# A two-layer decoder on one core: the last batch's shared expert and the first batch's way to transposed tokens move behind the conditional block

## The chip, the core and the metric

The kernel runs on one core of one Trainium2 chip as one launch. The metric is the device time of that launch in microseconds (us). A core has a matrix engine (PE, whose weight loads are listed apart as PEld), a vector engine (DVE), a scalar engine (ACT), GpSimd (POOL) and a queue engine that starts most transfers (SP). Each takes its instructions in the order in which they were written down for it, and waits where an instruction's input isn't there.

## The reference, cut to what matters

Four sequences (called batches here) of 512 tokens, 256 wide, go through two post-norm layers in float32:

```python
x = layernorm(x + L0_attn(x))            # attention over the 4 batches, 16 heads
x = layernorm(x + L0_xattn(x, ctx))      # one wide head against 1601 context rows
x = layernorm(x + L0_ffn(x))             # 16 experts, one for each token, and a shared expert
x = layernorm(x + L1_attn(x))            # causal, 16 heads of 16, rotary positions
x = layernorm(x + L1_xattn(x, ctx))      # 16 heads of 16 against the context
x = layernorm(x + L1_ffn(x))             # a soft decision tree of depth 8

def L0_ffn(x):
    logits = x @ w_router.T                          # 2048 tokens, 16 experts
    mask   = one_hot(argmax(logits))
    inputs = (sigmoid(logits) * mask).T[:, :, None] * x
    gate, up = split(inputs @ gate_up_proj)          # per expert, 256 -> 2 x 512
    routed = (up * silu(gate)) @ down_proj           # per expert, 512 -> 256
    shared = silu(x @ w_gate.T) * (x @ w_up.T) @ w_down.T   # every token
    return shared + routed.sum(over experts)
```

The change touches the third line, and the start of the fourth.

## The kernel before, in words

The program is three functions that run one after the other: `front()` (the first two lines of the model and the router), `experts()` (the third line without its norm) and `heads()` (that norm and the rest). Each builds a graph of nodes with `Plan.add` (`N` in the code) and calls `Plan.run`, a list planner. A node names an engine (or two, from which the planner chooses), an estimated cost, a due position, the nodes that it needs, and the buffers it takes and frees. The planner walks through its own estimated time; at each step it takes, among the nodes that can start soonest, the one with the smallest due position, and writes its instructions down. So it fixes the order on every engine before anything runs; on the chip only true data dependencies make an engine wait. Nodes that are named "none" hold a buffer; "dma" nodes stand for a transfer's time in the planner only.

In `experts()` the tokens are sorted by expert into tiles of 128 rows. 24 tiles (`NF`) are always done, in `sorted_tiles`. For each tile, three indirect transfers on POOL fetch the expert's weights (`wgu`, `wdn`) and the tile's token rows (`xs`); DVE scales the rows by the router's score (line 837), PE transposes them (842), ACT copies them out (249), PE multiplies by the gate and up weights, ACT takes the silu (857), DVE multiplies (859), PE multiplies by the down weights, ACT or DVE copies the result out and SP stores it to the DRAM array `ys_dram` (871). All multiplications go through the helper `mm` and carry its line, 245, so the tile names tell them apart: `xsT,wgu` and `wdn,he` are a tile's, `xT,w_sgu` and `w_sdn,hs` are the shared expert's.

The shared expert needs only the tokens: for each batch, eight multiplications into one PSUM bank each (`up`), four silus on ACT (798), four products on DVE (800), four multiplications (`down`), and four additions into the token rows `X` on DVE (808). All four batches are in the same graph as the tiles, with due positions 5.5 apart, and tile t is due at 0.2 + t.

Up to seven more tiles can be needed, depending on the router; they stand in a conditional block of their own behind the graph:

```python
            with tc.If(tiles[0] > NF):
                sorted_tiles(more, range(NF, NS))
                more.run(tc)
```

In the profiled execution the block is passed over; every engine still evaluates the branch (line 902).

`heads()` opens pools of its own for SBUF and PSUM, over the memory that `experts()` used. Its graph begins with `begin(b, pos)` for the four batches: four indirect transfers on POOL gather the tokens' expert rows from `ys_dram` by `dest` (1321), DVE adds `X` (1329), and `norm` normalizes them: statistics (1249, 1250), an inverse root by twelve small DVE instructions (`inverse_root`, 1234 to 1240), the norm into `XB` (1257), eight transposes on PE (1272), two copies into `XT`, and an addition of a bias row to `XB` on POOL (1278). From `XT` come the projections of each head group, rotary positions, a redistribution by SP transfers into `qT` and `kT`, and a first pass of scores for the row maxima (1106, 1108). Ahead of the heads the graph also clears buffers (`clear`, `ones_behind`), loads a pattern into the key buffers (`keys_of`, 962) and loads the tree's weights into the memory of `w_sgu` (`fetched`, 1420), where they stay in four of the ten buffers for exponentials (`raw`) until two small products have used them. All of these wait, in the planner, for batch 0's gathers to be issued or landed (`gathered`, `landed`).

Of the kernel before, what the change touches and what calls it, by code (L numbers as in the profile page):

```python
# [8 lines left out]
I32 = mybir.dt.int32  # L9
# [178 lines left out]
def act(n):  # L188
    return 0.1 + n * 0.833e-3


def dve(n):
    return 0.16 + n * 1.05e-3
# [11 lines left out]
def tile_decoder(ctx: ExitStack, tc: tile.TileContext, a, out):  # L205
# [37 lines left out]

    def mm(out, lhsT, rhs, c=0, n=1):
        nc.tensor.matmul(out, lhsT, rhs, start=c == 0, stop=c == n - 1)  # L245

    def copy(on, dst, src):
        if on == "act":
# [400 lines left out]
    def experts():  # L649
        plan = Plan()  # L650
        N, hold = plan.add, plan.hold
        with tc.tile_pool(name="mi", bufs=1) as mi, tc.tile_pool(name="mip", bufs=1, space=PSUM) as mip:
# [128 lines left out]
            sr = N("dve", 0.4, 0.0, sources, [so], free=[so])  # L781


            shared = [[] for _ in range(NB)]
            for b in range(NB):
                pr = 0.5 + 5.5 * b - (0.0 if b == 0 else 0.0)
                hs = hold("hs", pr)
                hid = []
                for f in range(4):
                    banks = []  # L790
                    for w in range(2):
                        def up(n, b=b, f=f, w=w):
                            for c in range(2):
                                mm(ONE[n.slot], w_sgu[:, c, w * F + f * P : w * F + (f + 1) * P], XT[b][:, c, :], c, 2)

                        banks.append(N("pe", cost_mm(1024), pr + f, up, [hs], take=["one"]))
                    s = hold("ss", pr + f)
                    e = N("act", act(512), pr + f, lambda n, s=s, p=banks[0]: nc.scalar.activation(
                        SS[s.slot], ONE[p.slot], AF.Silu), [s, banks[0]], free=[banks[0]])
                    hid.append(N("dve", dve(512), pr + f, lambda n, s=s, p=banks[1], hs=hs, f=f: nc.vector.tensor_tensor(  # L800
                        HS[hs.slot][:, f, :], SS[s.slot], ONE[p.slot], ALU.mult), [e, banks[1]], free=[banks[1], s]))
                for k in range(4):
                    def down(n, k=k, hs=hs):
                        for f in range(4):
                            mm(ONE[n.slot][:, :D], HS[hs.slot][:, f, k * P : (k + 1) * P], w_sdn[:, f, :], f, 4)

                    p = N("pe", cost_mm(1024), pr + 4 + k, down, hid, take=["one"], free=[hs])
                    shared[b].append(N("dve", dve(256), pr + 4 + k, lambda n, i=4 * b + k, p=p: nc.vector.tensor_tensor(
                        X[i], X[i], ONE[p.slot][:, :D], ALU.add), [p], free=[p]))


            gu_rows = a["L0_ffn_gate_up_proj"].rearrange("e p c n -> (e p) (c n)")
# [89 lines left out]
            with tc.If(tiles[0] > NF):  # L902
                sorted_tiles(more, range(NF, NS))
                more.run(tc)

    experts()


# [3 lines left out]
    def heads():  # L912
        plan = Plan()
        with tc.tile_pool(name="h1", bufs=1) as h1, \
# [41 lines left out]
            def ones_behind(n, t):  # L956
                nc.gpsimd.memset(t[:, :, :, HD : HD + 1], 1.0)
# [270 lines left out]

                return N("dve", 0.45, pe_, scaled, [r, cat], free=[po, rs]), cat

            def inverse_root(t, var):

                v, s, y = t[:, 0, :], t[:, 1, :], t[:, 2, :]
                nc.vector.tensor_scalar_add(v, var, EPS)
                nc.vector.tensor_single_scalar(y.bitcast(I32), v.bitcast(I32), 1, ALU.arith_shift_right)
                nc.vector.tensor_scalar(y.bitcast(I32), y.bitcast(I32), -1.0, 1597463007.0, ALU.mult, ALU.add)
                for _ in range(3):
                    nc.vector.scalar_tensor_tensor(s, y, -0.5, y, ALU.mult, ALU.mult)
                    nc.vector.tensor_tensor(s, s, v, ALU.mult)
                    nc.vector.scalar_tensor_tensor(y, s, 1.5, y, ALU.add, ALU.mult)  # L1240

            def norm(b, pos, y, parts, row=None):


                st, mv, sd = hold("lst", pos), hold("lmv", pos), hold("lsd", pos)
                stats = []
                for kq in range(4):
                    def stat(n, kq=kq):
                        nc.vector.bn_stats(ST[st.slot][:, kq, :], YY[y.slot][:, kq, :])  # L1249
                        nc.vector.bn_aggr(MV[mv.slot][:, kq, :], ST[st.slot][:, kq, :])  # L1250

                    stats.append(N("dve", 0.6, pos, stat, [parts[kq], st, mv]))

                rc = N("dve", 2.3, pos, lambda n: inverse_root(SD[sd.slot], MV[mv.slot][:, :, 1]), [sd, *stats], free=[st])
                norms = []
                for kq in range(4):
                    norms.append(N("dve", 0.47, pos, lambda n, kq=kq: nc.vector.tensor_scalar(  # L1257
                        XB[b][:, kq, :], YY[y.slot][:, kq, :], MV[mv.slot][:, kq, 0:1], SD[sd.slot][:, 2, kq : kq + 1],
                        ALU.subtract, ALU.mult), [rc]))
                plan.frees(norms[-1], [y, mv, sd])  # L1260
                if row is None:
                    for h in range(2):
                        i = 4 * b + 2 * h
                        N("sp", 0.4, pos, lambda n, i=i, h=h: nc.sync.dma_start(
                            out[i * P : (i + 2) * P, :].rearrange("(k p) d -> p k d", p=P),
                            XB[b][:, 2 * h : 2 * h + 2, :]), norms[2 * h : 2 * h + 2])
                    return
                xt = []
                for c in range(2):
                    def turn_x(n, c=c):  # L1270
                        for kq in range(4):
                            nc.tensor.transpose(ONE[n.slot][:, kq * P : (kq + 1) * P],  # L1272
                                                XB[b][:, kq, c * P : (c + 1) * P], ident)

                    px = N("pe", 0.46, pos, turn_x, norms, take=["one"])
                    xt.append(N("act|dve", (act(L), dve(L)), pos, lambda n, c=c, px=px: copy(
                        n.on, XT[b][:, c, :], ONE[px.slot]), [px], free=[px]))
                rw = N("pool", pool(1024), pos, lambda n: nc.gpsimd.tensor_tensor(  # L1278
                    XB[b], XB[b], rows[:, row : row + D].unsqueeze(1).to_broadcast([P, 4, D]), ALU.add), xt)
                added[b] = rw  # L1280
                return xt

            def finish(cross, b, pos, cats, cat):
# [16 lines left out]
                for h in range(2):  # L1300
                    def proj(n, h=h):
                        for kq in (2 * h, 2 * h + 1):
                            for c in range(2):
                                mm(ONE[n.slot][:, (kq % 2) * D : (kq % 2 + 1) * D], CT[ct.slot][:, c, kq, :], wo[:, c, :], c, 2)

                    po = N("pe", cost_mm(4 * D), pos, proj, cc, take=["one"])
                    prods.append(po)
                    a_ = N("dve", dve(512), pos, lambda n, h=h, po=po: nc.vector.tensor_tensor(  # L1308
                        YY[y.slot][:, 2 * h : 2 * h + 2, :], ONE[po.slot].rearrange("p (k n) -> p k n", k=2),
                        XB[b][:, 2 * h : 2 * h + 2, :], ALU.add), [po, y, added[b]], free=[po])  # L1310
                    parts += [a_, a_]
                plan.frees(prods[-1], [ct])
                return norm(b, pos, y, parts, R_W2 if cross else R_O2)
# [1 line left out]
            def begin(b, pos):  # L1315
# [3 lines left out]
                for kq in range(4):  # L1319
# [1 line left out]
                    g = N("pool", 0.98, pos, lambda n, i=i, kq=kq: nc.gpsimd.indirect_dma_start(  # L1321
                        out=YY[y.slot][:, kq, :], out_offset=None, in_=ys_dram,
                        in_offset=bass.IndirectOffsetOnAxis(ap=dest[:, i : i + 1], axis=0)), [y])
                    if b == 0:
                        gathered.append(g)
                    g = N("dma", 0.4, pos, None, [g])
                    if b == 0:
                        landed.append(g)
                    parts.append(N("dve", 0.44, pos, lambda n, i=i, kq=kq: nc.vector.tensor_tensor(
                        YY[y.slot][:, kq, :], YY[y.slot][:, kq, :], X[i], ALU.add), [g]))  # L1330
                return norm(b, pos, y, parts, R_O1)
# [1 line left out]
            def tree(b, pos, after):  # L1333

                parts = []
                for h in range(2):
# [58 lines left out]
                    if h == 0:  # L1395
                        y = hold("y", pos, [co])
                    a_ = N("dve", dve(512), ph + 0.1, lambda n, h=h, p=p: nc.vector.tensor_tensor(
                        YY[y.slot][:, 2 * h : 2 * h + 2, :], ONE[p.slot].rearrange("p (k n) -> p k n", k=2),
                        XB[b][:, 2 * h : 2 * h + 2, :], ALU.add), [p, y, added[b]], free=[p])
                    parts += [a_, a_]  # L1400
                norm(b, pos + 1.2, y, parts)

            added = [None] * NB
            gathered, landed = [], []
            done = [begin(b, 4.0 * b - 5.0) for b in range(NB)]
            cleared = N("pool", 1.5, -1.5, clear, gathered)
            emptied = N("dve", 0.6, -4.9, lambda n: nc.vector.memset(ACC[0], 0.0))
            keyed = keys_of(slice(0, L), 0.8, -3.0, landed)
            keyed2 = keys_of(slice(L, LC), 1.6, 3.0, landed)
            framed = [N("pool", 0.4, -1.5 + k, lambda n, k=k: ones_behind(n, VV[k]), gathered) for k in range(2)]  # L1410


            raw = [hold("pe", -5.0) for _ in range(4)]
# [5 lines left out]
                for k, w in enumerate(("w_fq", "w_fr", "w_flT", "w_fo")):  # L1419
                    nc.sync.dma_start(two(k), a[w].rearrange("(c p) n -> p c n", p=P))  # L1420

            fw = N("dma", 2.5, -1.0, None, [N("sp", 2.7, -1.0, fetched, [*raw, *landed])])
            tree_ready = []
            for k, dst in enumerate((w_gate, w_leaf)):
                def both(n, k=k):
# [124 lines left out]
```

## Time and profile before

| | |
|---|---|
| time, median of 3 runs | 1726.19 us (1723.04 to 1727.55) |
| the profiled execution, its own time | 1728.98 us |
| its span, first to last instruction | 1727.2 us |
| mean granted PE clock | 0.974 |
| PE busy | 1636.8 us (95%) |
| DVE busy | 1104.3 us (64%) |
| ACT busy | 759.5 us (44%) |
| POOL busy | 330.2 us (19%) |

`front()` runs to about 257 us, the tiles and the shared expert from there to 485 us, and `heads()` from there to the end. Times in the views are counted from the span's start. In a timeline row the first number is the start, the second the length of the merged group, and the bracket tells how long the engine was idle before it and what ended the wait. A PE multiplication of this kernel shows as two records.

### The profile page before, as it was taken

How to read it: one execution, taken by the hardware profiler on the slowest of the kernel's cores; microseconds unless marked ns; L12 is line 12 of the kernel's file. 1: busy time of each engine (PE TensorE's matmuls, PEld its weight loads, DVE VectorE, ACT ScalarE, POOL GpSimd, SP SyncE). 2: the span in 40 equal slices, each digit the busy share in tenths (PEclk: the TensorE clock that was granted, in tenths of full speed). 3: DMA queues.
4: the chain of work that ended last, by engine and by line, in shares of the span. 5: the costliest groups of instructions: out<-in, count | busy, mean ns of one | idle time of the engine just before them, and what ended most of it. 6: DMA issues, size and time to landing. Idle time of an engine off the chain costs nothing.

```text
span 1727.2 us, 28379 instructions
## 1 busy us (share of the span) xinstructions
PE 1636.8 (95%) x10756; PEld 856.2 (50%) x10756; DVE 1104.3 (64%) x2690; ACT 759.5 (44%) x1534; POOL 330.2 (19%) x503
## 2 busy tenths in 40 slices
PE   7889999999959999999999999999999999999995
PEld 4677776888834555545433334333334333343323
DVE  6998555111138876777866766776667766677715
ACT  0335551211112434434446556455554555545581
POOL 6652003432144544422000000100000000010000
PEclk8999999999979999999999999999999999999998
DMA  8101005886331000001000000000000100001000
GB/s 304 36 2 38 25 25 199 272 277 219 115 113 38 25 14 19 17 16 26 14 3 11 14 13 14 7 19 14 13 14 1 26 14 14 13 1 26 1 1 13
DMA packets 41275, 87.50 MB, mean 51 GB/s; under 512 B 7856, under 2 KB 26800, under 8 KB 38064
## 3 DMA queue, kind: packets, MB, share of 16 engines
q1 hardware_dynamic: 32304, 42.66, 9.1%
q0 software_dynamic: 8832, 43.00, 7.3%
q8 instruction: 86, 1.41, 0.3%
q14 instruction: 53, 0.43, 0.1%
HBM read 64.52 MB, written 8.26 MB: 42 GB/s over the span
## 4 chain that ended last, share of the span: by engine, by line
PE 65%; DVE 4%; ACT 1%; issue 1%; DMA 1%; POOL 0%; DVEq 0%; POOLq 0%; ACTq 0%
PE one L245 48%; PE acc L1190 14%; DVE junk L1108 2%; PE one L1210 1%; PE one L1142 1%; PE one L1272 1%; ACT w_sgu L1173 0%; PE one L1291 0%; DMA y<-ys_dram,dest 0%; DVE x L1257 0%; DVE lst L1249 0%; DMA ys_dram<-ye 0%; PE one L1381 0%; DVE y L1308 0%; DVE rt L1373 0%
## 5 line engine op out<-in xcount | busy, mean ns | idle before, releaser
L1106 DVE TENSOR_REDUCE mx<-one 128x1 f32<-128x512 f32 x768 | 486.4, 683 | 190.0 <-PE one L245 185.7
L245 PE MATMUL one<-qa,kT 32*128 32x512 f32 (+4 forms) x2176 | 515.4, 598 | 6.2 <-ACT w_sgu L1173 4.2
L245 PE MATMUL one<-kT,qT 32*128 32x512 f32 (+4 forms) x2560 | 502.2, 529 | 6.2 <-DVE mx L1106 2.6
L1173 ACT ACTIVATE w_sgu<-one 128x512 f32<-128x512 f32 (+2 forms) x510 | 278.6, 591 | 244.8 <-PE one L245 242.7
L245 PEld LDWEIGHTS one<-qa,kT 32*128 32x128 f32 (+1 forms) x2176 | 179.6, 182 | 204.3 <-issue 68.9
L245 PEld LDWEIGHTS one<-kT,qT 32*128 32x128 f32 x2560 | 190.6, 184 | 168.3 <-issue 47.9
L1190 PE MATMUL acc<-w_sgu,v 128*17 128x512 f32 (+4 forms) x1084 | 261.9, 566 | 0.0
L1173 ACT ACTIVATE pe<-one 128x512 f32<-128x512 f32 (+1 forms) x342 | 189.8, 602 | 102.2 <-PE one L245 101.6
L1278 POOL TENSOR_TENSOR x<-x,rows 128x1024 f32<-128x1024 f32 x12 | 28.3, 2361 | 808.3 <-PE one L1272 808.2
L1190 PE MATMUL acc<-pe,v 128*17 128x512 f32 (+1 forms) x748 | 179.5, 566 | 0.0
L1108 DVE CUSTOM_DVE_ANT_0 junk<-one,consts 128x128 f32<-128x128 f32 (+3 forms) x256 | 125.4, 490 | 35.1 <-PE one L245 12.0
L1190 PEld LDWEIGHTS acc<-w_sgu,v 128*17 128x17 f32 (+1 forms) x1084 | 34.2, 96 | 176.3 <-issue 162.8
L1173 ACT ACTIVATE w_sdn<-one 128x512 f32<-128x512 f32 (+2 forms) x172 | 89.9, 568 | 63.4 <-PE one L245 63.1
L245 PEld LDWEIGHTS e_one<-xsT,wgu 128*128 128x128 f32 x768 | 89.5, 192 | 3.8 <-issue 2.9
L245 PE MATMUL e_one<-xsT,wgu 128*128 128x128 f32 x768 | 89.6, 275 | 0.0
L1190 PE MATMUL acc<-w_sdn,v 128*17 128x512 f32 (+2 forms) x344 | 84.1, 568 | 0.0
L245 PE MATMUL one<-w_in,xT 128*128 128x512 f32 (+1 forms) x128 | 47.8, 527 | 13.5 <-DMA xT<-in_xT 12.2
L245 PE MATMUL e_one<-xT,w_sgu 128*128 128x512 f32 x128 | 59.8, 609 | 0.3 <-DVE lg L613 0.3
L859 DVE TENSOR_TENSOR he<-sg,e_one 128x512 f32<-128x512 f32 x24 | 16.5, 686 | 61.6 <-PE e_one L245 51.0
L555 ACT ACTIVATE pe<-one,nm 128x512 f32<-128x512 f32 x64 | 37.3, 596 | 27.4 <-DVE nm L547 27.3
L245 PE MATMUL one<-pT,ctxN 128*128 128x128 f32 (+1 forms) x416 | 49.0, 275 | 0.0
L245 PEld LDWEIGHTS one<-pT,ctxN 128*128 128x128 f32 (+1 forms) x416 | 48.2, 192 | 1.6 <-issue 1.2
(290 smaller groups left out, 2023.3 us busy)
## 6 DMA issues: line engine op xcount, KB each, us to landing
kT<-ku SPq DMA_DIRECT2D x64, 100.1 KB
qT<-qu SPq DMA_DIRECT2D x128, 32.0 KB
ctxN<-in_ctxN SPq DMA_DIRECT2D x4, 832.0 KB
ctxT<-in_ctxT SPq DMA_DIRECT2D x4, 800.5 KB
ys_dram<-ye SPq DMA_DIRECT2D x24, 128.0 KB
xT<-in_xT SPq DMA_DIRECT2D x16, 128.0 KB
x<-in_x SPq DMA_DIRECT2D x16, 128.0 KB
x_dram<-x SPq DMA_DIRECT2D x16, 128.0 KB
```

What stands on the lines that cost most here:

```text
L245: nc.tensor.matmul(out, lhsT, rhs, start=c == 0, stop=c == n - 1)
L555: nc.scalar.activation(PE_[w.slot][:, : k1 - k0], ONE[b.slot][:, : k1 - k0], AF.Exp, bias=NM[nm.slot][:, 1:2], accum_out=PS[sm_.slot][:, i ...
L859: h = N("dve", dve(512), pr, lambda n, s=s, p=banks[1], he=he: nc.vector.tensor_tensor(HE[he.slot].rearrange("p j t -> p (j t)"), SG[s.slo ...
L1106: nc.vector.tensor_reduce(MX[mx.slot][:, kq, j, m : m + 1], t, AX.X, ALU.max)
L1108: nc.vector.tensor_tensor_reduce(out=junk[:, : k1 - k0], in0=t, in1=m_qk[:, 384 - kq * P : 512], scale=1.0, scalar=NEG, op0=ALU.add, op1=A ...
L1142: nc.tensor.transpose(ONE[n.slot][:, kq * P : (kq + 1) * P], NM[nm.slot][:, kq].rearrange("p j r -> p (j r)"), ident)
L1173: nc.scalar.activation(PE_[e.slot][:kn, :w], ONE[s.slot][:kn, :w], AF.Exp, scale=HD**-0.5)
L1190: nc.tensor.matmul(ACC[acc.slot][32 * j : 32 * j + HD + 1, q0:], VV[v.slot][:kn, t, 4 * (g % 2) + j, :], PE_[exps[j ^ 2][0].slot][:kn, w : ...
L1210: nc.tensor.transpose(ONE[n.slot][:, kq * P : (kq + 1) * P], OO[o.slot][:, kq * P : (kq + 1) * P], ident)
L1272: nc.tensor.transpose(ONE[n.slot][:, kq * P : (kq + 1) * P], XB[b][:, kq, c * P : (c + 1) * P], ident)
L1278: rw = N("pool", pool(1024), pos, lambda n: nc.gpsimd.tensor_tensor(XB[b], XB[b], rows[:, row : row + D].unsqueeze(1).to_broadcast([P, 4, ...
```

## The change

Three things are done.

1. The shared expert's nodes become a function `shared_expert(plan, b, pr)`. The first graph of `experts()` calls it for batches 0 to 2, with due positions 7.5 apart in place of 5.5.
2. A third graph, `both`, is built behind the conditional block. It holds batch 0's gathers, norm, transposes and bias addition (what `begin(0)` and `norm` did in `heads()`) with the due position -1.0, writing into part of a weight buffer that is free by then, and the shared expert of batch 3 with due position 0.0 and up.
3. In `heads()`, `begin` runs for batches 1 to 3 only. Batch 0 has nothing left to wait for (`done[0]` is empty), and the clears and key patterns no longer depend on batch 0's gathers. The loads of the tree's weights depend, in the planner, on batch 1's transposed tokens instead.

```diff
-            shared = [[] for _ in range(NB)]
-            for b in range(NB):
-                pr = 0.5 + 5.5 * b - (0.0 if b == 0 else 0.0)
+            def shared_expert(plan, b, pr):
+                N, hold = plan.add, plan.hold
                 hs = hold("hs", pr)
...
+            for b in range(NB - 1):
+                shared_expert(plan, b, 0.5 + 7.5 * b)
...
             with tc.If(tiles[0] > NF):
                 sorted_tiles(more, range(NF, NS))
                 more.run(tc)
+
+            both = Plan()
+            for name, slots_ in plan.pools.items():
+                both.pool(name, len(slots_))
+            N = both.add
+            y = WGU[0][:, 0].rearrange("p (k d) -> p k d", d=D)
+            st, mv, sd = et("st0", [P, 4, 6]), et("mv0", [P, 4, 2]), et("sd0", [P, 3, 4])
+            stats, norms, xt = [], [], []
+            for kq in range(4):
+                g = N("pool", 0.98, -1.0, lambda n, kq=kq: nc.gpsimd.indirect_dma_start(
+                    out=y[:, kq, :], out_offset=None, in_=ys_dram,
+                    in_offset=bass.IndirectOffsetOnAxis(ap=dest[:, kq : kq + 1], axis=0)))
+                g = N("dma", 1.5, -1.0, None, [g])
+                g = N("dve", 0.44, -1.0, lambda n, kq=kq: nc.vector.tensor_tensor(y[:, kq, :], y[:, kq, :], X[kq], ALU.add), [g])
...
+                stats.append(N("dve", 0.6, -1.0, stat, [g]))
+            rc = N("dve", 2.3, -1.0, lambda n: inverse_root(sd, mv[:, :, 1]), stats)
+            for kq in range(4):
+                norms.append(N("dve", 0.47, -1.0, lambda n, kq=kq: nc.vector.tensor_scalar(
+                    X[kq], y[:, kq, :], mv[:, kq, 0:1], sd[:, 2, kq : kq + 1], ALU.subtract, ALU.mult), [rc]))
+            for c in range(2):
...
+                p = N("pe", 0.46, -1.0, turn, norms, take=["one"])
+                xt.append(N("act|dve", (act(L), dve(L)), -1.0, lambda n, c=c, p=p: copy(
+                    n.on, XT[0][:, c, :], ONE[p.slot]), [p], free=[p]))
+            N("pool", pool(1024), -1.0, lambda n: nc.gpsimd.tensor_tensor(
+                XB[0], XB[0], rows[:, R_O1 : R_O1 + D].unsqueeze(1).to_broadcast([P, 4, D]), ALU.add), xt)
+            shared_expert(both, NB - 1, 0.0)
+            both.run(tc)
...
-            added = [None] * NB
-            gathered, landed = [], []
-            done = [begin(b, 4.0 * b - 5.0) for b in range(NB)]
-            cleared = N("pool", 1.5, -1.5, clear, gathered)
+            added = [[]] * NB
+            done = [[], *(begin(b, 4.0 * b - 5.0) for b in range(1, NB))]
+            cleared = N("pool", 1.5, -4.9, clear)
             emptied = N("dve", 0.6, -4.9, lambda n: nc.vector.memset(ACC[0], 0.0))
-            keyed = keys_of(slice(0, L), 0.8, -3.0, landed)
-            keyed2 = keys_of(slice(L, LC), 1.6, 3.0, landed)
-            framed = [N("pool", 0.4, -1.5 + k, lambda n, k=k: ones_behind(n, VV[k]), gathered) for k in range(2)]
+            keyed = keys_of(slice(0, L), 0.8, -3.0, [])
+            keyed2 = keys_of(slice(L, LC), 1.6, 3.0, [])
+            framed = [N("pool", 0.4, -1.5 + k, lambda n, k=k: ones_behind(n, VV[k])) for k in range(2)]
...
-            fw = N("dma", 2.5, -1.0, None, [N("sp", 2.7, -1.0, fetched, [*raw, *landed])])
+            fw = N("dma", 2.5, -1.0, None, [N("sp", 2.7, -1.0, fetched, [*raw, *done[1]])])
```

`inverse_root` moves to the top of the program unchanged, so that both places can call it.

## The prediction

> **What bounds the kernel now.** On the page PE is busy 95% of the span, DVE 64%, and 65% of the chain that ended last is PE: whatever keeps PE working is hidden, and only PE's holes, or PE time that becomes a hole, can move the end. First view: the chain of waits around the border between `experts()` and `heads()`.
>
> ```profile
> 485.20 3.63 DMA ys_dram<-ye
> ...
> 492.74 6.87 DMA y<-ys_dram,dest
> ...
> 504.56 0.14 issue
> 504.69 2.21 PE one L1272 x8
> 506.90 17.64 PE one L245 x64
> ```
>
> Between the last tile's store and the transposes of batch 0 there is no PE in the chain. Second view, busy time by stretch (span, then PE, PEld, DVE, ACT, POOL with instruction counts, granted clock, DMA share, GB/s):
>
> ```profile
> 324.00:344.00 20.00, 18.90 (x140) 17.88 (x138) 3.70 (x8) 3.56 (x8) 8.78 (x10) 1.00 0.84 278
> 464.00:484.00 20.00, 20.00 (x132) 18.58 (x131) 4.17 (x8) 2.59 (x6) 0.00 (x0) 1.00 0.04 15
> 484.70:504.70 20.00, 0.03 (x2) 0.04 (x1) 7.04 (x27) 0.37 (x1) 6.15 (x10) 0.64 0.61 209
> ```
>
> PE is full up to 484.7 and then idle for 20 us. The expert stage itself is PE-bound: its ten stretches of 20 us from 284 on have 197.1 us of PE in 200. Third view, the timeline: prices and releasers.
>
> ```profile
> 291.55 1.88 PE L245 MATMUL e_one<-xT,w_sgu 128*128 128x512 f32 x4
> 335.42 1.99 PE L245 MATMUL e_one<-wdn,he 128*128 128x256 f32 x8 [1.10 <-DVE he L859]
> 482.83 1.89 PE L245 MATMUL e_one<-wdn,he 128*128 128x256 f32 x8
> 490.22 0.95 POOL L1321 DMA_INDIRECT y<-ys_dram,dest  x1 [36.49 <-issue]
> 500.64 0.39 DVE L1329 TENSOR_TENSOR y<-y,x 128x256 f32<-128x256 f32 x1
> 504.69 2.21 PE L1272 MATMUL one<-consts,x 128*128 128x128 f32 x8 [19.97 <-DVE x L1257]
> 506.77 3.78 PE L245 MATMUL one<-xT,wq 128*128 128x512 f32 x4
> ```
>
> Fourth, two rows that tell how pools change hands: the longest waits, and the start of `experts()`.
>
> ```profile
> POOL ones L690 <- DVE best L619: 45.8, 1, 45.8
> 257.22 3.78 PE L245 MATMUL e_one<-xT,w_sgu 128*128 128x512 f32 x4 [0.32 <-DVE lg L613]
> ```
>
> The memset of `ones` has no input, yet it waited for the last DVE instruction of the stage before; the first PE instruction likewise for the copy that emptied the last bank. So a new pool's first writes wait for the old pool's last users.
>
> **Part by part.** T0 is the end of PE's work in the expert graph (before: 484.72, which is 482.83 + 1.89).
>
> *Taken out of the expert graph:* batch 3's shared expert. One `up` bank takes 1.72 us (from 291.55 to the next PE start, 293.27), eight take 13.8; the four `down` take 7.0 (284.37 to 291.34 for 32 records). Together 20.7 us of PE in a PE-bound stage: T0 becomes 464.0. Its four silus (0.60 each) and eight DVE instructions (0.69 and 0.42) lie beside PE, before and after.
>
> *What that filler covered.* Due positions 7.5 apart leave tiles 4 to 11 with little but tiles. There the trace has the like: seven tiles between 319.64 and 364.22, with only two `down` (3.5 us) between them, took 44.6 us for 7 x 5.51 of tile work (0.21 + 3.57 + 1.73): PE idled 2.2 us, in 1.1 us pieces as at 335.42, where DVE stood behind a late `xs` transfer. Eight such tiles give 2.5 us, and the last tile, whose silu and product nothing covers any more, about 1 (before, a `down` stood there). From above: if every filler-free tile took the 6.37 us of that stretch, 8 x 0.86 + 1 = 7.9; from below 0.5. DMA is no floor: 24 tiles of 1.84 MB and 2 MB of late weights at the 277 GB/s of that stretch are 167 us, from 275 to 442. I take 3: T0 = 467.0.
>
> *The branch.* PE's compare-and-branch of line 902 lasted 3.46 us, to 485.6, hidden in the hole. Now PE has work behind it, so 0.9 us show. If PE were held until 489.3, as SP was (T0 + 4.6), `up` would end at T0 + 18.4, 1.4 after the first norm that the next step finds: the wait there would vanish and the end move by under 1 us.
>
> *The new graph.* I follow the planner by its costs. Eight `up` fill PE until 13.75 in its time; gathers, additions, statistics, root, one product that slips in, and norms make the transposes ready at 14.7; the `down` need the fourth product, 15.4. So PE's order is eight `up`, two transposes, four `down`, and then `heads()`. On the chip: `up` ends at T0 + 0.9 + 13.8 = 14.7. The gathers can't come sooner after T0 than now: the store lands at +4.1, the first issue is at +5.5, the fourth at +9.3. They landed 6.9 us after issue, beside 3.4 MB that SP had started at 489 to 494; the gathers issued alone at 504.82 and 515.99 were used 2.7 and 3.0 later. SP's loads go into the new pool, whose first writes now wait until the shared expert has read its buffers, so I take 3.0 (bounds 2.7 and 6.9): +12.3. From the last addition to the last transpose was 6.26 us (500.64 to 506.90), plus 0.7 for the product, minus 0.5 since PE isn't cold: +18.7. PE waits 2.3 us for the first norm, and behind it stand the four `down` and all of `heads()`: +25.7.
>
> *Clock.* After the 2.43 us without PE work at 249.28 the granted clock was 0.50 from 252 until 261; after the hole the first four projections took 3.58 us to the next start, not 1.72. A wait of 2.3 us with half-empty transposes behind it looks like the first: 1.9 us more (0 from below), +27.6. The first projection waits for the last addition out of the old banks, 0.5: S = T0 + 28.1.
>
> The Trainium skill ("TensorE: Matmul & The Clock Gate", Part 1: The HAM clock gate) has PE throttled only after an idle window of about 3.4 us. By that the 2.3 us wait would leave the clock at full speed and the result would be 1.9 us lower; the trace speaks against it, with 0.50 after 2.43 us.
>
> *Balance at the start of `heads()`.* Before, 506.77 is T0 + 22.1. Now T0 is 20.7 - 3 earlier and S is 6.0 later: 11.7 us gained.
>
> *Moved past other queues.* Batch 0's four gathers, 20 small DVE steps, eight transposes, two copies and the 2.35 us bias addition are the same instructions. On POOL that addition now stands before the clears and batch 1's gathers; it ends by T0 + 21.1, before S, and costs nothing. But POOL's clears (2.0 us), batch 1's gathers and SP's key patterns, which ran inside the hole, now start at S beside the first projections. Their cover is the way from the first projection to the first scores, 17.7 us (506.77 to 524.45); that is now 1.9 shorter by the warm clock, and POOL's clears and first gather end about S + 3.7, where the first rotary product came at 4.6. What is late is batch 1: its tokens were transposed 19 us after the heads' first projection, and its transposes, its projections and the tree's two products (which the planner now puts behind it) filled PE's waits before 550. Without them at hand: 3.8 us of tree products and as much of projections, at most 7.6; at best the shorter way gains 2. I take a loss of 2.5, nearer the low end, as PE idled only 2.4 us there. The root's move and the lists change nothing.
>
> Sum: 11.7 - 2.5 = 9.2 off 1728.98, or 1719.8 in the profiled execution; its time was 2.8 above the median, so 1717.0.
>
> **Rivals.** (a) *The holes I priced don't open*: full clock through the wait, 0.5 lost in the stage, 1 gained at the heads' start: 9.2 + 1.9 + 2.5 + 3.5 = 17.1, giving 1709.1. For it: most tiles run without a gap even at 5.5 us. Against: the 0.50 after 2.43 us.
>
> (b) *SP's loads still meet the gathers*: landing 6.9, S 3.9 later but without more cold, about 3.4: 1720.4. For it: key buffers lie mostly over weight buffers that are free early. Against: the `ones` row.
>
> (c) *The filler was needed*: 7.9 lost in the stage and 5 at the start: 11.7 - 4.9 - 5 = 1.8, giving 1724.4, no change that can be told. For it: DMA share 0.84 to 0.89 in the sparse stretch.
>
> (d) *Slower: the exponentials' buffers.* Four of ten stay held until the tree's two products, now behind batch 1's tokens. Four exponentials go together, so with six buffers only two of the next four can run ahead: two wait, 1.2 us by their 0.60 each, three times a causal group, some 3.5 us. Before, the products ran at 521.77 and 530.65, the first exponential at 550.8. The loss decides once five groups run before the second product: 17.5 us, 1717.0 + 17.5 = 1734.5. Against: batch 1's tokens were there 23 us before that exponential.
>
> That the change doesn't do what it says isn't open: the graph is emitted behind the branch and PE has nothing else there.
>
> **The numbers.** A measurement of this kernel tells about 0.3% from no change, 5.2 us: 1721.0 to 1731.4. Forecast 0.47, (a) 0.20, (b) 0.11, (c) 0.13, (d) 0.09. Faster 0.78, same 0.13, slower 0.09. Time 1717.0. The best of all bounds is 11.7 + 1.9 + 2.5 + 2 = 18.1, or 1708.1; the range starts a little below and goes up to 1726.0, beyond (c), leaving out (d) and the edges.
>
> **What would show it.** T0 near 467; no idle stretch of 20 us, but one of 1 to 4 us before the eight transposes at T0 + 17; 32 records of `w_sdn,hs` right behind them, the first at half clock; gathers landing 3 us after issue; SP's key loads after the last `down`; the first head projection near 495. Wrong if T0 is above 473 (rival c), if gathers take 6 us (b), or if PE's waits in the first four head groups grow by over 8 us (d).

## The result, and the profile after

The changed kernel took 1719.6 us (median of 20 runs, lowest 1712.77), the kernel before 1727.55 (20 runs beside them). The ratio is 0.9957, with a 95% interval of 0.9941 to 0.9972: 7.4 us faster, by 4.8 to 10.2. One of the 20 runs took 3060.89 us and is left out of the ratio. Two later sets of runs of the same unedited file gave 0.9946 each. The forecast was 1717.0, with "faster" as the likeliest outcome. Of the 2.6 us between the forecast and the median, 1.4 are the kernel before, whose median was 1726.19 when the forecast was made. So the sum is nearly right. Its terms are not, as the rest shows: up to the first head projection the change gains 4 to 6 us more than forecast, and in the heads it loses 2 to 6 us more.

The profiled execution of the changed kernel took 1731.54 us (span 1729.8), which is longer than the one of before (1728.98, span 1727.2). Read alone, it would say "slower". Where its time went is the third part of this section.

**The border.** The chain of waits of the changed kernel (start, duration, what):

```profile
470.68 13.97 PE e_one L245 x32
...
485.53 6.92 PE e_one L245 x32
...
492.47 2.63 DMA kT<-in_keys
```

Where the chain of before had 20 us of store, gathers, additions and norms, it now has PE from 470.7 to 492.5. The timeline of PE shows what the three pieces are (start, duration, engine, line, operation, tiles, shapes; in brackets the idle time before it and what ended it):

```profile
467.11 1.99 PE L245 MATMUL e_one<-wdn,he 128*128 128x256 f32 x8 [0.85 <-DVEq L915]
470.68 13.97 PE L245 MATMUL e_one<-xT,w_sgu 128*128 128x512 f32 x32 [1.58 <-PEq L915]
484.49 1.04 PE L947 MATMUL e_one<-consts,x 128*128 128x128 f32 x8
485.36 7.07 PE L245 MATMUL e_one<-w_sdn,hs 128*128 128x256 f32 x32
493.00 1.96 PE L245 MATMUL one<-xT,wq 128*128 128x512 f32 x4 [0.56 <-issue]
```

T0 is 469.10 (467.11 + 1.99). The branch leaves 1.58 us open; then batch 3's eight `up`, the eight transposes of batch 0 without any wait, the four `down`, and the first head projection at T0 + 23.9. The 19.97 us hole is gone. The transposes could follow at once because the gathers were early, as the timeline of POOL and DVE shows:

```profile
472.28 0.95 POOL L929 DMA_INDIRECT wgu<-ys_dram,dest  x1 [30.84 <-issue]
477.55 0.43 DVE L933 TENSOR_TENSOR wgu<-wgu,x 128x256 f32<-128x256 f32 x1 [0.20 <-DMA wgu<-ys_dram,dest]
```

The first gather is issued at T0 + 3.2, not at T0 + 5.5 as before. The last norm ends at 484.41, just before the eighth `up` does (484.65).

**The first groups of heads.** Part of the gain is given back here. First the timeline of PE and DVE, then busy time by stretch (span; PE, PEld, DVE, ACT, POOL with counts; granted clock; DMA share; GB/s):

```profile
502.28 0.42 DVE L1365 TENSOR_TENSOR y<-y,x 128x256 f32<-128x256 f32 x1 [4.03 <-DMA y<-ys_dram,dest]
506.25 3.17 DVE L1365 TENSOR_TENSOR y<-y,x 128x256 f32<-128x256 f32 x1
511.00 0.67 DVE L1056 TENSOR_TENSOR rt<-one,consts 128x512 f32<-128x512 f32 x1
511.73 1.63 PE L245 MATMUL one<-kT,qT 32*128 32x128 f32 x4 [0.91 <-DVE rt L1056]
515.60 0.79 PE L245 MATMUL one<-kT,qT 32*128 32x128 f32 x2 [2.24 <-DVE mx L1159]
```

```profile
505.00:510.00 5.00, 4.61 (x14) 1.71 (x14) 4.86 (x6) 0.69 (x1) 3.97 (x5) 1.00 0.23 61
510.00:515.00 5.00, 2.44 (x11) 0.71 (x6) 4.56 (x18) 0.00 (x0) 1.26 (x1) 0.72 0.21 51
515.00:520.00 5.00, 4.40 (x12) 2.76 (x12) 4.50 (x15) 0.00 (x0) 2.41 (x3) 0.50 0.79 240
...
525.00:530.00 5.00, 5.00 (x25) 3.29 (x23) 3.15 (x12) 1.17 (x2) 3.28 (x2) 0.50 0.11 26
```

DVE is written down to do batch 1's additions ahead of the second rotary product (`rt`, line 1056) and the first maxima (`mx`, line 1159). It waits 4.03 us for the first gather, one addition takes 3.17 us, and PE, which has nothing else, waits 0.91 and 2.24 us for what stands behind. Batch 1's gathers now run beside SP's loads, and the second of them takes as long to land as batch 0's did before (chain of waits of the change):

```profile
497.29 6.87 DMA y<-ys_dram,dest
```

The granted clock falls to 0.50 between PE's two waits: 0.72 over the window from 510 to 515 means 2.8 us at half, so the fall is at 512.2. It lasts until 532.7, though PE is not idle at all after 515.6. The two waits cost 3.2 us; the clock costs more. Summed over the first 60 us after the first head projection (windows of 4 us; PE's busy time times one minus the granted clock), the clock took 12.4 us of PE's work in the changed kernel and 3.4 before, and PE idled 3.7 and 2.5 us. The difference is 10.2 us; the fourth group of heads is 10.8 us later than before, counted from the first projection. Up to group 15 the same sum, taken over the stretches at half clock, is 12.5, 16.8 and 14.1 us in the three profiles of the change and 5.2 before, while PE's waits are 8.6, 8.7 and 7.8 us and 7.8 before: what the heads lose is half clock.

What sets that half clock off is not shown. In the third profile of the change (`after_third`, busy time by stretch and timeline of PE) the clock falls at 507.1, 0.15 us after PE's long wait has begun, and PE had not waited for over 0.1 us since the first head projection at 488.72:

```profile
507.00:508.00 1.00, 0.00 (x0) 0.00 (x0) 0.84 (x5) 0.00 (x0) 0.17 (x1) 0.55 0.02 2
509.69 2.91 PE L245 MATMUL one<-kT,qT 32*128 32x128 f32 x8 [2.74 <-DVE mx L1159]
```

So the long wait isn't what brings the clock down there. Ahead of the fall PE runs the first scores, multiplications of 32 rows (`32*128`); whether these count is not tested.

**A spell of half clock.** The head groups 15 and 16 take 40.72 us from one to the next in the profile of before and 50.04 in this one. The same stretch in the profile of before, of the change, and of a second execution of the changed kernel:

```profile
830.00:840.00 10.00, 9.43 (x86) 5.81 (x86) 8.47 (x18) 1.79 (x5) 1.71 (x6) 1.00 0.09 12
```

```profile
830.00:840.00 10.00, 10.00 (x31) 3.69 (x27) 6.85 (x14) 0.97 (x2) 0.29 (x1) 0.50 0.26 45
```

```profile
830.00:840.00 10.00, 9.67 (x81) 5.97 (x82) 8.60 (x18) 2.31 (x5) 0.59 (x2) 1.00 0.35 56
```

In the second fence PE is as busy as in the others and does less than half as many multiplications. The three profiles of the unedited change show the spell in two cases and not in the third, with the same instructions in the same order. It costs 9.3 us, and that is why this profile is the longer one. All later profiles are therefore compared by stage:

| us | last `wdn,he` ends, from the stage's start | first head projection, from there | head group 1, from the projection | group 4 | group 15 | 15 to 16 | span |
|---|---|---|---|---|---|---|---|
| before | 227.8 | 22.1 | 59.5 | 111.5 | 308.4 | 40.7 | 1727.2 |
| after | 210.2 | 23.9 | 68.2 | 122.3 | 314.0 | 50.0 | 1729.8 |
| after_again | 208.5 | 24.2 | 66.2 | 121.2 | 317.3 | 40.7 | 1723.8 |
| after_third | 208.1 | 24.2 | 65.9 | 119.9 | 313.2 | 50.1 | 1724.9 |
| tokens_only | 228.5 | 16.8 | 64.1 | 119.0 | 310.9 | 40.7 | 1732.2 |
| shared_only | 208.3 | 39.7 | 59.7 | 111.5 | 307.2 | 50.1 | 1735.7 |
| tree_early | 209.8 | 23.9 | 61.8 | 116.8 | 311.0 | 40.7 | 1717.5 |
| tree_early_2 | 208.4 | 24.0 | 62.1 | 117.1 | 311.3 | 40.7 | 1716.0 |
| gather_5 | 209.1 | 24.2 | 60.5 | 116.8 | 313.6 | 40.7 | 1719.1 |
| tree_gather_5 | 208.9 | 23.9 | 56.7 | 109.6 | 308.2 | 46.8 | 1720.0 |
| tree_gather_5_2 | 207.7 | 23.9 | 59.2 | 112.0 | 312.1 | 40.7 | 1714.6 |
| spacing55 | 209.1 | 26.1 | 65.8 | 119.9 | 313.1 | 50.1 | 1730.3 |

The stage's start is DVE's copy of the router's logits (line 613 before, 624 after), the end of a `wdn,he` record is T0, and a head group is marked by its reciprocal of the row sums (`rs`). For the profile of the change the table adds up so: 2.0 later at the stage's start, 15.8 gained up to the first projection, 5.6 lost up to group 15, 9.3 in the spell, 1.5 after group 16: 2.6 longer. For the second execution: +2.8, -17.1, +8.9, 0 and +2.0: 3.4 shorter.

### The profile page after: what moved, and what is told of

Same layout as the page of the kernel before. It is cut to its first block, busy times and chain, and to the rows that moved or that the text cites. A ratio compares the mean times of both kernels' runs of the same rounds, so it can differ in the third digit from the quotient of the medians.

```text
span 1729.8 us, 28387 instructions
## 1 busy us (share of the span) xinstructions
PE 1655.4 (96%) x10756; PEld 863.2 (50%) x10756; DVE 1101.9 (64%) x2690; ACT 758.9 (44%) x1534; POOL 330.5 (19%) x503
## 4 chain that ended last, share of the span: by engine, by line
PE 66%; DVE 4%; ACT 1%; issue 1%; DMA 1%; POOL 0%; DVEq 0%; ACTq 0%
PE one L245 48%; PE acc L1241 14%; DVE junk L1159 1%; PE e_one L245 1%; PE one L1261 1%; PE one L1193 1%; PE one L1312 1%; PE one L1331 0%; ACT w_sgu L1224 0%; DMA y<-ys_dram,dest 0%; DVE y L1365 0%; DVE lst L1289 0%; DVE x L1297 0%; DVE y L1348 0%; DVE rt L1408 0%
## 5 line engine op out<-in xcount | busy, mean ns | idle before, releaser
L245 PE MATMUL one<-kT,qT 32*128 32x512 f32 (+4 forms) x2560 | 515.2, 539 | 8.2 <-DVE mx L1159 3.0
L1224 ACT ACTIVATE pe<-one 128x512 f32<-128x512 f32 (+2 forms) x342 | 184.6, 587 | 105.6 <-PE one L245 104.7
L1241 PE MATMUL acc<-pe,v 128*17 128x512 f32 (+2 forms) x748 | 174.1, 551 | 0.0
L1159 DVE CUSTOM_DVE_ANT_0 junk<-one,consts 128x512 f32<-128x512 f32 (+3 forms) x256 | 125.4, 490 | 44.5 <-PE one L245 22.6
L1224 ACT ACTIVATE w_sdn<-one 128x512 f32<-128x512 f32 (+2 forms) x174 | 96.4, 600 | 67.4 <-PE one L245 67.1
L1241 PE MATMUL acc<-w_sdn,v 128*17 128x512 f32 (+3 forms) x352 | 90.6, 594 | 0.0
L245 PE MATMUL e_one<-xT,w_sgu 128*128 128x512 f32 x128 | 59.2, 609 | 1.9 <-PEq L915 1.6
L245 PE MATMUL e_one<-wdn,he 128*128 128x256 f32 x192 | 45.9, 382 | 5.1 <-DVE he L872 4.3
L245 PE MATMUL one<-ctxT,q 128*128 128x512 f32 (+1 forms) x128 | 49.4, 518 | 0.0
```

Of the source, the lines that this page charges most:

```text
L1159: nc.vector.tensor_tensor_reduce(out=junk[:, : k1 - k0], in0=t, in1=m_qk[:, 384 - kq * P : 512], scale=1.0, scalar=NEG, op0=ALU.add, op1=A ...
L1224: nc.scalar.activation(PE_[e.slot][:kn, :w], ONE[s.slot][:kn, :w], AF.Exp, scale=HD**-0.5)
L1241: nc.tensor.matmul(ACC[acc.slot][32 * j : 32 * j + HD + 1, q0:], VV[v.slot][:kn, t, 4 * (g % 2) + j, :], PE_[exps[j ^ 2][0].slot][:kn, w : ...
```

## The experiments

**The change again.** The unedited file was run beside the first experiments and once more beside the last.

> The changed kernel once more, nothing edited, for a second profile and a second measurement. My theory: the gain at the heads' first projection (15 to 16 us against before, counted from the start of the expert stage) and the loss in the first four head groups (5 to 9 us) come back in every profile, since they follow from the written order; the 9.3 us that the first profile of the change lost between head groups 15 and 16, and 1.8 us at group 29, do not come back, since the order there is like the one of before; the time is 0.2 to 0.7% under the kernel before. Rival: the step at group 16 is a property of the new order; then it is there again with 9 us and the span is again about 1730.

> The changed kernel unedited, on the same chip as the next two, so that they can be compared: 0.4 to 0.6% under the kernel before. If half-clock spells come by chance, its profile shows 40.7 or about 50 us between the ends of head groups 15 and 16, and nothing between by more than a partial spell.

Measured: 1721.98 against 1728.42 (0.9946, 0.9926 to 0.9966), and 1717.94 against 1727.95 (0.9946, 0.9921 to 0.9971). T0 and the first projection came back within 2.1 and 0.3 us, the late first group too (66.2 and 65.9). The spell between groups 15 and 16 was gone in one and there in the other, so the written order alone doesn't bring it.

**Each half alone.** The first keeps the new graph for the tokens only; the shared experts are all where they were.

```diff
-            for b in range(NB - 1):
-                shared_expert(plan, b, 0.5 + 7.5 * b)
+            for b in range(NB):
+                shared_expert(plan, b, 0.5 + 5.5 * b)
...
-            shared_expert(both, NB - 1, 0.0)
```

> Batch 0's way to transposed tokens is in the graph behind the branch as in the change, but all four batches of the shared expert stay in the first graph, 5.5 apart as before. My theory (the filling of PE's hole is what gains): PE ends the expert graph where it did before, idles about 14 us instead of 20, since the gathers meet no loads and start sooner, and then the first head groups lose what they lose in the change: 5 us gained, 5 to 9 lost, the time within 0.3% of before or slightly above. Rival (the early, quiet gathers are the gain and the shared expert's place does not matter): 0.4% under before, like the change.

Measured: 1730.42 against 1728.42 (1.0002, 0.9981 to 1.0022): nothing. The timeline of PE in `tokens_only`:

```profile
505.38 2.21 PE L947 MATMUL e_one<-consts,x 128*128 128x128 f32 x8 [13.91 <-DVE x L942]
508.26 3.51 PE L245 MATMUL one<-xT,wq 128*128 128x512 f32 x4 [0.68 <-ACT xT L260]
```

The hole is 13.9 us instead of 20, as nothing fills it, and the heads start with half clock. Of the 5.3 us won from T0 on, 2.4 are lost up to group 15 (7.6 at group 4) by the heads, which have the order of the change; the rest is within what the interval leaves open.

The second moves only the shared expert; batch 0's gathers stay in `heads()`, with the old dependencies.

```diff
-            y = WGU[0][:, 0].rearrange("p (k d) -> p k d", d=D)
...
-                XB[0], XB[0], rows[:, R_O1 : R_O1 + D].unsqueeze(1).to_broadcast([P, 4, D]), ALU.add), xt)
             shared_expert(both, NB - 1, 0.0)
...
-            done = [[], *(begin(b, 4.0 * b - 5.0) for b in range(1, NB))]
+            gathered, landed = [], []
+            done = [begin(b, 4.0 * b - 5.0) for b in range(NB)]
```

> Only the shared expert of batch 3 is in the graph behind the branch; batch 0's gathers and norm stay in the graph of the heads as before, with the old waits in the planner. My theory (a new pool's first writes wait for the old pool's last users): the gathers, whose target lies in the heads' pool, can't start before PE has read the last buffer of the shared expert, about 22 us after the expert graph's end; the 16.5 us from first gather to first projection then stand bare again, PE idles 15 to 17 us, and nothing is gained: within 0.3% of before, or up to 4 us slower. Rival (no such wait): the gathers start 3 to 6 us after the expert graph's end and are hidden beside the shared expert: about 10 us faster than before.

Measured: 1736.98 against 1728.42 (1.0031, 1.0007 to 1.0054), slower. T0 is as early as in the change, but the gathers wait (timeline of PE and POOL):

```profile
482.93 7.07 PE L245 MATMUL e_one<-w_sdn,hs 128*128 128x256 f32 x32
490.76 0.95 POOL L1332 DMA_INDIRECT y<-ys_dram,dest  x1 [50.86 <-DVE x L818]
505.18 2.21 PE L1283 MATMUL one<-consts,x 128*128 128x128 f32 x8 [15.18 <-DVE x L1268]
```

The first gather goes out at T0 + 23, released by the shared expert's last addition into `X` (line 818): it writes into the pool that follows. The 21 us of PE work moved behind the tiles only push the hole back. Counted from the stage's start, the first head projection comes 1.9 us earlier than before here, 4.6 in `tokens_only`, and 15.8 to 17.6 in the change: each half is there to let the other lie beside it. In time the two halves are worth 0 and -0.3% alone and +0.5% together. The hole doesn't explain the -0.3%: this profile is 3 us ahead of before at group 15, and it is longer by the spell (50.1) and by 2.3 us ahead of the stage. Whether the other runs of `shared_only` lose their time in the same way is not shown.

**The loss in the heads.** The theory after the result was that DVE's order makes PE wait there and that the clock multiplies it: the tree's two products, which PE had between 520 and 532 before, now come at 540 and 548, and batch 1's additions stand ahead of the first maxima, since the planner counts 0.4 us for a gather that lands 6.9 after its issue. Two edits, each for one of these, and both together:

```diff
-            fw = N("dma", 2.5, -1.0, None, [N("sp", 2.7, -1.0, fetched, [*raw, *done[1]])])
+            fw = N("dma", 2.5, -1.0, None, [N("sp", 2.7, -1.0, fetched, [*raw])])
```

> The change, but the loads of the tree's weights no longer depend on batch 1's tokens in the planner (only on their buffers), so they are issued with the key patterns and the two tree products can fill PE's first waits again, as before. My theory of the loss at the heads' start (PE lacks work there, idles and falls to half clock): 2 to 5 us faster than the change, first head group's end 3 to 6 us nearer to its start. Rival (DVE's order is the cause: batch 1's additions and norm stand before the rotary product and the first maxima): no more than 1 us from the change.

> The tree edit alone, again. If its first measurement (0.85% under before, interval 0.51 to 1.19) holds: 3 to 5 us under the change on this chip. Rival (that measurement, with six undisturbed runs, was on the lucky side and the edit is worth what its trace shows up to head group 15, 3 us in one profile and 6 in the other): 1 to 6 us; nothing if its half-clock spells are more frequent.

```diff
-                    g = N("dma", 0.4, pos, None, [g])
+                    g = N("none", 5.0, pos, None, [g])
```

> The change, but in the planner the gathers of batches 1 to 3 take 5.0 us to land (a pure delay) in place of 0.4 us on the planner's transfer engine; nothing else is edited. Theory A (DVE's order: the additions of batch 1 stand at the head of DVE's queue and wait for gathers that land 3 to 7 us after issue, with the rotary products and the first maxima behind them): the first scores and maxima come sooner, PE's waits of 1.5 and 2.2 us between 509 and 516 shrink, and the time is 2 to 5 us under the change's. Theory B (what PE lacks is work: the tree's two products): within 1 us of the change's.

> Both edits together: the tree's loads free of batch 1's tokens, and 5.0 us for the gathers of batches 1 to 3 in the planner. Theory A: 2 to 4 us under the kernel with the tree edit alone, so some 1.1% under the kernel before, with the first head group ending 59 to 60 us after the first projection as before the change. Theory B: the same as the tree edit alone, 0.85% under before.

> Both edits, again. By its trace (head group 15 ends 308.2 us after the first projection against 314.0 and 317.3 for the change, the rest alike but for spells) it should be 6 to 9 us under the change. By its first measurement (0.59% under before) 1 us. If the second holds again, the gain of the first head groups is given back by half-clock spells later in the heads, which its profile should show as a mean clock no higher than the change's.

Measured, each against the kernel before on its chip: `tree_early` 1718.64 against 1728.42 (0.9915, 0.9881 to 0.9949) and 1717.75 against 1727.95 (0.9933, 0.9908 to 0.9959); `gather_5` 1722.39 against 1731.66 (0.9948, 0.9929 to 0.9966); both together 1719.68 against 1731.66 (0.9941, 0.9917 to 0.9965) and 1716.75 against 1727.95 (0.9933, 0.9908 to 0.9958).

Both edits bring group 1 forward. It comes 4 to 6 us earlier with the tree's products early, 5 to 8 with the gathers' time told, 7 to 12 with both, where it is as early as before the change or earlier. In `tree_early` the products lie where PE has work to do anyway, and the wait for `rt` remains; with both edits two waits of 1.4 us remain, 2.2 and 1.4 in the repeat (timelines of PE, first `tree_early`, then `tree_gather_5`):

```profile
508.99 1.89 PE L245 MATMUL one<-w_sgu 128*128 128x256 f32 x8
515.91 2.99 PE L245 MATMUL one<-kT,qT 32*128 32x128 f32 x10 [3.00 <-DVE rt L1056]
```

```profile
515.16 0.69 PE L245 MATMUL one<-kT,qT 32*128 32x256 f32 x2 [1.44 <-DVE mx L1159]
517.26 3.13 PE L245 MATMUL one<-kT,qT 32*128 32x256 f32 x4 [1.41 <-DVE mx L1159]
```

Summed as above over 60 us, the clock took 12.4 us in the change (11.7 and 12.8 in its repeats), 10.0 in `tree_early` and in its repeat, 8.9 in `gather_5`, and 4.4 and 8.1 with both. But the time does not follow group 1. `gather_5` was expected to gain a few us and gained nothing over the change (0.9948 against 0.9946 and 0.9957): its group 15 is no earlier (313.6 against 313.2 to 317.3), so what it wins up to group 1 is given back by the fifteenth. The traces show where. From group 1 to group 15 PE waits 6.9 us in `gather_5` against 4.7 to 5.6 in the three profiles of the change, and the half clock takes 5.1 us of its work against 0 to 4.9; what is left is 241 us in each. Both edits together were expected at 1.1% below before and reached 0.6 to 0.7%: there PE waits 7.9 us in this stretch in both profiles, and the half clock takes 3.4 and 5.0. `tree_early` and the two together beat the kernel before in each of their four measurements; against the change on the same chip they were 3.3, 0.2 and 1.2 us lower, and their intervals overlap with the change's. That they are the fastest versions is likely and not settled.

**The spacing of the filler.**

```diff
-                shared_expert(plan, b, 0.5 + 7.5 * b)
+                shared_expert(plan, b, 0.5 + 5.5 * b)
```

> The change with the due positions of the three remaining shared experts 5.5 apart as before, in place of 7.5. My step: the stage loses about 3 us for lack of filler between the tiles; with 5.5 the filler is used up earlier and the last tiles run bare, where each costs 0.5 to 1.4 us more. Expected: the expert graph ends 0 to 4 us later, and the time is within 0.3% of the change's. Rival (the filler's place is worth nothing): no difference at the graph's end beyond 0.5 us.

Measured: 1719.6 against 1731.66 (0.9937, 0.9913 to 0.9961), not slower than the change. The expert stage ends at the same time (209.1 against 208.1 to 210.2). So the two spacings make no difference to the stage that can be told. The first projection is 2 us later after T0 here, and the timeline of PE shows why:

```profile
470.69 15.67 PE L245 MATMUL e_one<-xT,w_sgu 128*128 128x512 f32 x32 [2.10 <-PEq L915]
```

PE waited 0.85 us, multiplied for 2.0 us (the last `wdn,he`), and waited 2.10 us at the branch. Then the granted clock was 0.50 for 3.4 us, from 471.9, and the eight `up` took 15.67 us in place of 13.97.

## Why the prediction was right or wrong, point by point

*The filler taken out.* Right. 17.7 us were forecast (20.7 - 3); the stage is 17.6, 19.3 and 19.7 shorter in the three profiles, so the holes cost 3.1, 1.4 and 1.0. The stage's end in `shared_only` (208.3) and `spacing55` (209.1) says the same. Rival (c), with 7.9 lost in the stage, is out; the 5 us that it had lost at the start of the heads did come, for another reason (below).

*The branch.* Forecast 0.9 us open; measured 1.58, 1.88 and 1.85. Too small by up to 1.

*The new graph's order* was as derived: eight `up`, the transposes, four `down`, the heads.

*The gathers.* This is the first step that failed: "The gathers can't come sooner after T0 than now". They came at T0 + 3.2 instead of 5.5, because the last store landed sooner, 1.7 us after its issue by the list of transfers, where the chain of before had 3.63; why it landed sooner is open. With that the norms were ready before the eighth `up` was done, and the wait of 2.3 us and the cold clock behind it, 1.9, had no place. The first projection came at T0 + 23.9 to 24.2 instead of 28.1: 4 us better than forecast. The landing itself was sized rightly (3.0; measured 2.8):

```profile
wgu<-ys_dram,dest POOLq DMA_INDIRECT x4, 2.8
```

Rival (b) is out with it. SP's first key pattern starts at 492.47, when the last `down` ends, as the row on the memset of `ones` had let one expect; `shared_only` shows the same rule on POOL, at the price of a whole hole.

*The clock at the border.* Rival (a) said full clock, and the granted clock is 1.00 from 464 to 500. But the wait that the forecast thought would drop it didn't occur, so the change itself doesn't tell whether a wait of 2.3 us would have done so. `spacing55` does: with 2.10 us at the branch the clock fell, and the `up` took 1.7 us longer, near the 1.9 that was charged. In the heads it fell to 0.50 with waits of 0.91 and 2.24 us on the two sides of the fall. The Trainium skill ("TensorE: Matmul & The Clock Gate", Part 1: The HAM clock gate) has the gate close after an idle window of about 3.4 us and open after about as long of sustained work. Here no single gap was that long, and the clock stayed at 0.50 until 532.7, 17 us after PE had become busy without a gap. In both directions the measurement differs from the page.

*The start of the heads.* This is the second step that failed, and the term of the sum that was most mis-sized: "I take a loss of 2.5, nearer the low end", with 7.6 as the most. Group 1 is 6.4 to 8.7 late and group 15 4.8 to 8.9. The mechanism was named (batch 1 late, the tree's products behind it, PE without work in its waits), but it was priced as PE work at full clock. The waits themselves grew by 1.2 us only (3.7 against 2.5 in the first 60 us); what grew was what the half clock took, by 9.0. The forecast charged the clock once, at the border where nothing happened, and not here. It had read a row that holds such a price: 0.50 from 252 until 261, ten microseconds for a 2.43 us gap. Nor did it charge batch 1's gathers, which it had start beside SP's loads, with the 6.9 us that rival (b) had for batch 0's.

*Rival (d)*, the exponentials' buffers. Its order shows: six exponentials run, from 537.44, and the seventh comes at 548.54, behind the tree's first product at 540.42, where before ten ran in a row from 550.80. But PE doesn't stand still for it: its waits over the first four groups are 5.2, 5.3 and 4.4 us in the three profiles against 4.3 before, not 8 more. A second, shorter half clock, 539.5 to 546.4, falls into this place; whether the order has to do with it is open.

*The sum.* Forecast 11.7 - 2.5 = 9.2; measured, in the three profiles of the change and with the spell left out, 6.7, 3.4 and 11.7, which have 7.3 for their mean and agree with the 7.4 to 9.3 of the ratios. They differ by the heads (4.8 to 8.9 lost) and by what lies before the stage and after group 16, where the change does nothing (3.5, 4.8 and 1.1 lost). That the total was nearly right is luck: the two errors are of about one size.

## What to carry to other kernels

Work that is moved into a hole pays only together with what lets it lie beside the hole's chain: here the filler alone brought the heads' first projection 2 us forward, the early gathers alone 5, and the two together 16 to 18. When a stage's start is shifted, look at the granted clock behind it and not only at the waits: here the half clock took 9 us more there and the waits 1.2. One profile against one profile can have the wrong sign when a spell of half clock falls into one of them: compare by stage, and see whether the same instructions take another time.

## What the hardware showed that was not expected

The spell: about 20 us at a granted clock of 0.50 with PE busy 10.00 of 10 us, in some executions and not in others of the same file, 9.3 us each time it is whole. In the 12 later runs of the change that came beside the last experiments, four took 1726.6 to 1731.5 us at a mean clock of 0.964 to 0.968 and eight 1712.5 to 1719.1 at 0.972 to 0.976; the kernel before has the same tail (1733.4 to 1739.1 at 0.965 to 0.969, against 1725.0 to 1729.2 at 0.972 to 0.974, and one run between). That it is the same spell in each of these runs is likely and not shown, as only the profiled ones show its place.

The twelve profiles narrow down what sets it off. In each of them PE has one wait of 0.57 or 0.58 us in this stretch, 20.0 us after the mark of group 15; in the profile of the change the row behind it is

```profile
827.59 4.27 PE L245 MATMUL one<-kT,qT 32*128 32x65 f32 x41 [0.58 <-ACT w_sgu L1224]
```

In each trace the granted clock changes only at whole steps of 3.413 us from its other changes. In the five profiles with the spell the wait begins 0.49 to 1.08 us after such a step; in the seven without it, 0.07 to 0.34 or 2.69 to 3.31 us after one. So the same instructions meet the spell or not with the place at which they fall between the clock's own steps, in all twelve without exception. No run shifted them on purpose.

An addition on DVE took 3.17 us instead of 0.42, from 506.25, while POOL ran two rotary products:

```profile
506.64 1.28 POOL L1058 TENSOR_TENSOR qu<-q,consts 128x512 f32<-128x512 f32 x1
507.86 1.27 POOL L1058 TENSOR_TENSOR ku<-q,consts 128x512 f32<-128x512 f32 x1
```

It ended 0.3 us after the second. The Trainium skill ("SBUF — State Buffer", SBUF: two separate sides) tells of one pair of ports that the two engines hold in turn for a whole instruction, and the length agrees. By these records the addition had begun 0.4 us before the first product, but inside an indirect transfer that POOL ran ahead of it (505.52 to 506.48). The addition before it shows the plain case:

```profile
504.11 1.26 POOL L1060 TENSOR_TENSOR ku<-ku,rt 128x512 f32<-128x512 f32 x1 [2.17 <-DVE rt L1056]
504.19 1.46 DVE L1365 TENSOR_TENSOR y<-y,x 128x256 f32<-128x256 f32 x1 [0.23 <-DMA y<-ys_dram,dest]
```

It began 0.08 us into a POOL product and ended 0.28 us after it; in `after_third` an addition that began at 498.90, 0.23 us ahead of a product, took 0.41. No run was made to take the two engines apart.
